# A four-layer graph network on one core: another fixed order for every engine, bound checks inside the work graph, and one input load moved behind four adjacency tiles

## The chip, the cores and the metric

The kernel runs on one core of one Trainium2 chip. The metric is the device time of one execution in microseconds. A core has five engines that run their own instruction queues: the tensor engine (PE in the profile, its weight loads PEld), the vector engine (DVE), the scalar engine (ACT), GpSimd (POOL) and the sync engine (SP), which here only issues transfers. An engine works its queue in the order in which the program was written; a semaphore makes an instruction wait for another engine or for a transfer. Three runs of the kernel before took 4156.73, 4158.40 and 4158.55 us; the median is 4158.4 us.

## The reference

The input `x` is 16 batches of 1024 nodes with 256 features in float32; `adj` is one 1024 x 1024 integer adjacency matrix for all batches. Four layers follow each other, and each adds to `x` what it computes from `relu(layernorm(x))`:

```python
h = jnp.maximum(_layernorm(x, axis=-1), 0.0)
x = x + _L0_gnn_ref(h, adj, L0_gnn_W, L0_gnn_a)   # graph attention, 1 head, relu
...
x = x + _L1_gnn_ref(h, adj, L1_gnn_W, L1_gnn_a)   # graph attention, 1 head, elu
...
x = x + _L2_gnn_ref(h, adj, ...)                  # dot-product attention, 8 heads of 32, masked, then norm, feed-forward, norm
...
x = x + _L3_gnn_ref(h, adj, L3_gnn_W, L3_gnn_a)   # graph attention, 4 heads of 64, elu
```

In a graph attention `e[i,j] = leaky_relu(src[i] + dst[j])`, with `src` and `dst` from `h W a`; where `adj` is zero the weight is none; a softmax over `j` then weights `h W`. Layer 2 takes the scores from queries and keys instead.

## The kernel before

**Tiles.** A batch's 1024 nodes are 8 tiles of 128 (`NT`), in two halves of 4 (`NH`, `TH`). Stages are pairs of layer and batch, 64 in all; the list `order` (L1845 to L1850) runs layer 2 of one batch beside layers 1, 3 and 0 of others, so that stages with different needs overlap.

**The softmax without its maximum.** Exponentials are taken straight, as sums and products of `exp` of source and target. That is right as long as the values stay within bounds. The kernel therefore collects sums and minima in small tiles (`gat_seen`, `inv_seen`, `degree`, `below`), compares them with the bounds after all work (L1990 to L2004), and adds up the broken ones in `bad`. Every engine then loads `bad` into a register (L2013) and jumps over a second, general implementation (`tc.If(found > 0)`, L2014), which runs only where a bound was broken.

**The work graph.** No engine's order is written in the code. `op(...)` (L810) makes a node with its engine, a planned cost in us, a rank, the function that emits its instructions, the nodes it comes after, and the buffers (`Hold`) that it takes and ends. The tensor engine's nodes that the prediction speaks of are these; behind each stands its tile name in the profile:

- `scores` of `dot_item` (L1595, tile `sc`): four products of 32 rows side by side, one per head; planner form 132. It takes two of three pairs of PSUM banks (`"u": Ring(3)`, L967).
- `values` (L1628, `acc<-pe`) and `totals` (L1658, `sums<-pe`) of `dot_item`, `values` and `totals` of `pair_item` for layer 3 (L1477 `acc<-p`, L1502 `sums<-p`): four products of 32 columns side by side; form 32.
- all others use the whole array, form None: `values` of `gat_item` for layers 0 and 1 (`av`), projections (`pm`), transpositions (`tp`, `tps`, `tpo`, `tpv`, `tpr`, `tp_mask`).

Between `scores` and `values` lie two exponentials on ACT (L1613) and two products with the mask on DVE (L1621). Before `totals`, GpSimd issues a transfer that adds one tile of weights onto another (L1647, `pe<-pe`). In the feed-forward of layer 2, GpSimd computes each row's `rstd` (L1054, L1055), ACT scales (L1758), and PE transposes (`tp<-y`).

**The planner.** `forward` (L842) plays the graph: for each engine, `choose` (L824) looks at all nodes that could begin, and among those that could begin within `SLACK` = 0.5 us of the earliest takes the one of the lowest rank. Costs, hand-over delays (`DELAY`) and the cost of a change of PE form (`SWITCH`) are constants. The ranks come from the table `RANKS`, three characters for each node; `play` (L944) uses it where its length fits the number of nodes, and otherwise plans from the ranks in the code:

```python
            if len(RANKS) == 3 * len(ops):
                digits = [DIGITS.index(c) for c in RANKS]
                best = forward([(x * 90 + y) * 90 + z for x, y, z in zip(digits[::3], digits[1::3], digits[2::3])])
```

The nodes' functions are then called in the played order, and that is the order in which each engine's queue is written.

**The first transfers.** SP issues the two halves of batch 0, the eight adjacency tiles of 512 KB each (L724), then the two halves of batch 1 (L725), then weights.

Of the kernel before, what the change touches and what calls it, by code (L numbers as in the profile page):

```python
# [26 lines left out]
F32 = mybir.dt.float32  # L27
BF16 = mybir.dt.bfloat16
U8 = mybir.dt.uint8
I32 = mybir.dt.int32  # L30
AF = mybir.ActivationFunctionType
ALU = mybir.AluOpType
# [15 lines left out]
    "#+;#TX#$I#U9#U3#&X#%h#WX#)4#Wc#&>#$b#U)##w##W$5o##o##Z##D##b#$'#$-##t##$#$:##r##y##G##Q#$F#$>#/4#$N#$R##x#%-#%^"  # L48
    "#$o#'S#'T#&F#&a#%g#&$#'%#&{##T#$|##?##@#%F#SZ##B#%+##>##S#$f##c##M##a##L##]##9##v##i##z##|##u##^#$@#$)##n#$0#$4"
    "##U#oi#-@##V#sX##F##X#$^##=##_#%e##P#)h##{#$<##q#$`#/3#$&#$P##m#$3#$8#$J#$,#$9#$K#$1#*e#%r##%##j#$a#&4$0;#Cy$0r"  # L50
    "#RB#Cx#%|#']#**#&@#)g#([#'q#%m#&]#&7#%v##8#$=##}#$G##-#$L#$_#$j#$M##)#$E##p#$]$$T#'?#%a$Mo#%5#$n#$U#%L#%9#%}#%R"
    "##(#$C#%%#$c#%8##Y#&L#%7#xt#%S#'V#]n#%l#$5$%C#%V#%E#0W#%0##l#&+#$i#&,#%n#(o#)v#)V#D,#%t#$v#$r#$S#%$#%##%'#$O#$d"
    "#$H#$6#)z##4#K5#$+#&I#%?#%Y#(8#YI#(A#<Z#$A#&;#$l#%x#&1#Au#$7#(s#%,#$;#%.#%T#%z#%O#&:#DW#d-#&Q#&A#)W#%s#'H#DU#'P"
    "#'E#&0#(2#(I#(4#'r#*d#e6#&=#,6#k8#&m$Fk$Pc#($#$x#>b#$w#$Z#%3#5Q#$T#&8$@{##J#%X##O#Gr#({#%:#'K#$h#&c#'8##,#&[#%="
    "#T+#$u#&`#V9#%&#'-#%*#JZ#SB#%/#%i##C##5#%w#us##2##H##N#$s#$.#$k##e##;#$e#')#%P#&l#%<##d#$*#$##vC#%K#XB#*|#$B#%G"
    "##A$/b#&6##1#%`#&D#((#%]#%I#%{#&%##0#%_#%Q#&9#&##&)#D=##7#FF$&r#&C#%d#&.##6#)0#&B#+4#O)##3##[#&Y#%@#&g#;b$&?#e'"
    "#4O#%2#&Z#&*#(y##/#%j$/i#&&#'&#di#&p#&/#&f#&M#&|#'.#('$5w#'*#(%#&N#$2#'6#&3#&d#&R#&K#&U#&o#&V##.#DD#&E#&q#M9#'="
    "#&<#&n#eH#'D#',#w'$0(#'X#'C#&z#'J#&h#'@$6t#U@#'[#';#'A#%;#(-#'x#a}#DE#kw#'W#%p#'_#N[#&r#(>#Sm#&u#)G$.4#)P$.3#&e"
    "$Ip#'d#ma#tD#);$Pa$Ph$PQ$K?#&i#'I#&s#'N#&v#'2#&j#%A$D+#&P#&H#0A#%k#(D$JC#'p#'>#'a#&x#&_$JO#G;#O/#'5#'L#%1#'k#0>"
    "$78#(P#ip#'e#'7#kv#P)#d`$Ms$1j#'g#(G#Pd#(l#)@#(E$?$#(c#0.#'w#'s#(p#'G#)E#'}#''#(^#(&#'|#(6#UK#(/$@J#'#$@O#'y#()"  # L60
    "#ku#$Q#'v#$/#Il#.W#B1#(:#(.$>1#)3#4/#Ix#4.#(5#(L$;V$>D##k#(1$9##'u#))#(d#)%#)^#*=#)_#)t##g#'R#'j#(##(,#'U#(9#'i"
    "#(n#(B#(V#(W#&'#(*#'m#*n#)8#)1#(}#;4#)y$$:#(x#C,#(i#(Y#(h#(_#(z#)m#(U#&?#)b#(g#(k#*K#(j$*_#(f#J@#*2#)F#Ah#,[$*9"
    "#*,#*7#-z#<c#)*$LG#)=#)<#++#)M#*:#-(#(v#)B#*+#)i#:q#*1#+9#2y#)?#)Q#+J#)D$$z#*3#,,#*}#)p#)U#;Y#'h#)a#$Y#+<#*9#)S"
    "#)[#*##)$#*&#*R#+%#*H#)w#*[#,r#->#*`#+-#.S#)(#)c#)O$$u#)#$+S#s|#)R#),#/M#)+#,f#*G#+H#*p#*c#(H#*%#*E#*8$,R#*a#*4"
    "#*V#*-#+0#Q5#*k#,U#*q#+*#*@#(@$OJ#*l#-$#*j#*M#)u#qU#+N#,B#*y#K%#-g#+L#*f#*O$P,#*N#*r#+(#*_#)n#,u#j{#-'#+5#+1#IV"
    "#*o#+f#*t$3%#,k#.##h6#+?#'1#-,#,I$2J#,j#+e#L}#,b#+x#+8$2)#E7#nl#kn#+O#+##+K#-D#S{#CK#+u#Oy#)l#,*#+>#+Y$<|#+V#CP"
    "#+t#+i#.M$6O#.C#sD#,$#sv$;[#,N#+`$C?#AC#-k#?L#,'#+z#,T#:M#+D#A<#,F#,>#Os#jT#,J#00#+{#g?#+|#)r#+q#+m#+/#*]#1F#,7"
    "#/[#*U#L^#,+#q<#+X#-+#,8#.`#,3#/)$-($E##-[$F@#D$#-a$8s#Hh#-w$*S$-z#-p#.B#E##-##.u#Ob$GE#F]#+C#8u#qs#.O#.T#-u#L+"
    "#-&#.e#;g#/1#,<#.*#ej#n.#)|#j7#,}#-{#.%#-B#]z#-S#-H#-E#-G#.2#)s$#Z#.(#.c#-Z#GY#a5#/G$Ng#-b#/g$Hu#,)#.i#=.#kT#A&"
    "#gi#,&$Ch#ef$D)$Kp#,Y#8h#-f#,i#,2#-t#*<$Cj#(|#,L#,1$Cs#yr#'0#.Z#,^#8g#/U#-2#,4#'<#/##/P$MP#,o#,Z#-m#ym#2H#g=#,{"  # L70
    "#*C#/d#-O#,]#-K#+&#.-#+W#-1#,l#+o#)o#.{#,##-<#,x#-i#+S#-I#-%#/Q#+}#01#)j#-F#-3#-l#.d#*w#.K#.h$;=$/D#-`#-?$F,#.]"
    "#,X#.g#,A#-_$F)$EL$FB$A=#-o#o8#.q#.&#-N$5r$EI$FC#._#-r#-e#W[#(w#.9#)x#-d#/J$/B#-:#,Q#WZ#}i$P7#)J#-Y#-s#9m#)X#2)"
    "#-7#.N#)`#KW#-U#'l#-V#-0#,?#-x#.I#RQ#,v#/?#.>#.$#.j#.'#.A#-}#.l#/%#.V#/o#.?#-X#./#.<#.b#05#/'#``#.=#-6#'(#+h#2|"
    "#MH#-8#.7#/e#.U#g)#/f#.x#15#/s#/2#.^#,K#/I#,W#,M#Ha$P`#g[#yg#,a#/`#.v#.Y#04#/q#/;#,m#/W#.X#+v#/@#+y$K>#+r#/b#It"
    "#,s#,t$'z#0r$GX#.:#,w#,_#,z#.8#+P#-;#9-#-J#-W#Yt#.m#0S#Ys$>x$(]#.y$9$#)f#+M#$[#(r#,5#*.#*)#,P#*?#*A#,R#$W#*F#*I"
    "#*J#*Q#*>#9e#*P#)9$Kf#+6#nk#+3#+'$3l$F0#+Q#*T#,D#(`#+,#,O#(;#+$#-A#,V#h/#-.#*^#*S#*g#*{$L{#)K$3Y#)T#+a#+n#+=$)E"
    "#+I#+g#+E#+2#+[#Ba#8G#,-#>R#)6#)5#+)#-|#,@$3n#.,#.R#.6#.J$N;#.H#.G#-n#.f#;y#/$#<&#1M#]b#/5#UU#/>#.Q#.t#).#`W#]T"
    "#/Z#zN#0+#-]#*z#/m#1%#/.$7:$Nv#/}#,H#1U$EV#/O#/E#Nt#/z$(B#0&#,:#,S#*$#D5#/u#0x#C/#0i#0{$-f$Mm#-v#u'$+[#'$#0M#0L"
    "#/_##'#N<#I[#.z#3w#):#0;$?F#0(#0P$8h#NP#DY$PU#/,$@X#/t#.}#::#YZ#+R#0'#0n#/h#/v#0F#+G#/=#HG#32#03#/j#C_#/i#-j#0I"
    "#/S#18#/^#/T#3?#.5#1C#z,#HS#0?#0o#6w$-0#1A#61#1k$;Q#1$#0u#0q#/y#/<#1m#1N#0m#/B#0<#0,#2L#26#0##0l#0J#0B#14#0|#/F"  # L80
    "#0]#0V#0[$+k#0O$+f#0a#3n#.+#/D#.w#06#/p#Xr#29#0H#0%#08#0)#0G#0`#0=#0Z#0:$Nn#0y#0k#0e#1,#KY#09#0d#0z#/A#2J#fr#-9"
    "#19$8`#2a#1_#sA#1B#0h#1D#1@#2=#2b#6u#1:#1`#1G#6v#7<#/K#0X#4I$+n#0/#1T#0g#1>#1-$+`#0b#1i#1e#2E#1o#/]$8q#4H#1=#3U"
    "#1}#/c$8K#sh#s?#0K#1W$)u#2C#21#+@#1p#1;#1f#1H#A*#1Q#16#1<#1j#1I#tY$*s#2q#2I#1O#1z#2w#1x$?9#3##/(#1t#1)#1+#1?#2<"
    "#3B#3&#ZZ#2Q#1l$I6#1h#2i#1c#2B#1q#4(#2/#2j#2m#2R$K;#6(#2t#2%#1J#2x#4'#3K#2K#Y1#0t#3c#57#/n#2W$-8#2$#3N#22#1L#3)"
    "#<O#/l#2c#2;#kZ#4D#2_#5A#3M#:u#2D#4F#27#1R#2+#<N#5@#3:#2S#<z$I0$?'#3F#4C#4b#0D#88#2{$Iv#2}#0Q#3>#z0#2z$O'$O&#3$"
    "#4>#39$'1#2e#:s#3/#3j#38#3e#3=#4k#35#4=#3J#5e#3h$5E#4|#Et#+d#*;#3a#2@#5Y#4x#3b#2,#1Z#3Q#4c#4q#79#5T#5'#11#4@#4d"
    "#66#7J#5F#4S#3d#3[#4a#4?#7E$L>#7)#4p#4W#4e#5($;1#;q#6k#5)#23#3+#5$#1n#4i#5d#4^#3y#5;#5^#6H#5h#4-$>P#'B#2'#0_#6h"
    "#0*#4+#3T#3-#<6#37#<v#1a#4g$/'#2##3_#3G#=+#Kb#2Z#{?#2d#4l#nv#2[#4,#2g#4n#:t#56#3W#4J#<r$:C#5>#1b#3(#3.#4L#I=#3{"
    "#N{#3g#l?#7T#59#1^#9;#SA$Iw#2:#58#30#64#13#6Y#12#2^$/*$-7#5i#3l#3Z#8x#2F#7/#1{#*X#3v#/k#1]#8|#1($:x#3`#]k#6]#2X"
    "$JG#2O#6X#2v#3X$9<$.q#2M#07#1[#5E#@Y$)i#tL#ie#40#3C#wv#34#02#3s#T'#3I#4v#3;#3i#2P#0w#5,#2V#x^#3p#77#3O#2]#6P#5P"  # L90
    "#4M$'S#43#7'#4U#0p$,{#4*#6'#3V#3}#3o#4y#5/#2r#5o#5n#5D#6S#3S#5}#5Z#6A#4K#50#5<#67#48#5B#3L#6:#3r#3D#3]#4;#3R#6%"
    "#+j#4f#5_#^{#5H#44#5:$--#4T#33#-R#81#5V#5p#7##^$#3H#41#8;#4t#6L#5y#4m#6-#62#6W#6Q#5k$PR#7N#53#5M#$q#83#2o#5|#2p"
    "#6{#yp$J/$$P#6t#7Q$J0#6M#5S$,]#3u#6s#7H#6+$&=#5`#6K#qc#54#4X#6}#74#|L#6d#Vy#4%#4$#3P#3x#aM#5-#4`#5L#yP#4j#46#j)"
    "#4:#4R#4Z$6p#4{$%>#4P#4z#4##6_#2f$:$#4h#4&#31#5K#4o#5U#6E$Cv#Fk#4w#5w$Np$2&#3f#4G#^z#5g#5m$8a#:T#68#6^#7?#4Y#5W"
    "#45#4E#47#|5$JS#}U$@H#8}#5[#5?$Be#6*#5O$-'#8D#5%#5v#78#5z#2u#9J#7`#6F#6/#6B#}|#5q#rq#70#Ld#87#6N#6J#7$#6r#3m#6x"
    "#+w#6$#6.#6o#76#yf#f>#6b#6l#ww#7(#6O#1S#5a#6f#7%#6e#6[#5f#1Y#7*#73#8-#5X#10#6>#7=#7@#7;#6;#1E#6m#7G#6?#7-#7d#7,"
    "#71#8V#6y#7k$@8#8_#82#91#8$#7l#7Z#7W#[S#7|#8L$51#8[#8I#8`#8i#8m$4M#8^#8W#8P#9,#9W#8c#8p#8##6D#:##8:#Yk#:R$Hn#9&"
    "#<@#9+$2_#;F$+q#V'$D6#8O#<<#?+#??#7S#7q#6U#7I#ET#7U#7]#5s#6j#7V#+p#5N#7b#7R#7}#9)#84#7c#8C#8F#8t#8&#7z#65#7s#7["
    "#7K#7X#7n#*x#6&#7w#7o#9*#7g#EK#8A#8%#6i$(D#7t#7L#6|#8<$&A#-C#8q#8X#,;#6z#8=#8R#8l#7m$J1#9$#>j#Ea#8(#6@#4V#rP#4B"
    "#?=#TB#7r#7P#80#8.#8k#9A#72#9=#8a#8z#9g#Dz#9r#8B#7p#:?#86#'O#9h$%U#:2#tM#-/#8b#8M#9:#:0#8n#9}#&-#Sz#.[#'9#9'#:1"  # L100
    "#t)#;|#(C#Y<#(X#8o#9b#9]#96#9N#9I#;p#9n#8/#8,#;Z#;9#=y#;P#:L#<,#;L#='#4}#9i#9<#9`#(q#=M#WJ#<|#94#(e#9D#9f#6q$Ot"
    "#6p$QC#6Z#:U#7>#9a#W@#:|#8r#m;#8Y#:(#95#9u#8]#:z#8s#9P#{.$(A#9x#=b#:*#7F#8Z#89#8j#9^#7^#8{#8Q#9T###$*-#;*#;8#>)"
    "#@f#>J#5u#@%#8S#7Y#>0#;z#:C#P-#98#;@#<B#9H$Ht#:-#7u#:p#:O#9@#(Z#:%#:=#:A$5b#:.#9V#75#;V#52$%J#zi$B'#:Y#9_##I$-`"
    "##<##&#:H#9t#9q#<V#9M$'J#:G#n]#:o#:c#&w#9U#:`#9/#:_#:Q#:9#9[#:]#8v#jt#:Z$3f$-&#?]#:y#'+#:@#k)#;H#k/#9p#:;#;'#)Z"
# [518 lines left out]
def fast_path(tc, bad, x, adj, l0_w, l0_a, l1_w, l1_a, w_qkv, ln1_g, ln1_b, ln2_g, ln2_b, w1, b1, w2, b2, l3_w, l3_a, out):  # L623
# [13 lines left out]
    with ctx:  # L637
# [186 lines left out]
        def choose(open_ops, time, begin, key, slack):  # L824
# [14 lines left out]
            open_ops[best[1].eng].remove(best[1])  # L839
            return best  # L840

        def forward(rank):  # L842

            time, form, held = [0.0] * 6, 0, {DVE: 0.0, POOL: 0.0}
            ready = [0.0] * len(ops)
# [1199 lines left out]
```

## Time and profile before

| what | value |
|---|---|
| median of three runs | 4158.4 us |
| the profiled execution, its own time | 4158.92 us |
| its span, first to last instruction | 4157.2 us |
| granted PE clock, mean | 0.996 |
| PE busy | 4080.8 us (98%) |
| DVE, ACT, POOL busy | 3123.5, 2316.4, 1255.7 us |
| first PE instruction; last of the layers | 8.63 us; ends 4140.87 us |
| last DVE instruction of the layers | ends 4145.10 us |
| `bad` written | 4148.44 us |

The profile gives each engine's instructions with start and length, what ended the idle time before each, and the names of the tiles. A float32 product appears as two matmul records, so `scores` and `values` are eight records each. Records of PE overlap, and their ends are modelled; the time that an item takes is therefore read from start to start, from its first record to the first of the next item. Queue instructions, such as branches, loads of a register and drains, do not count as busy.

### The profile page before, as it was taken

What the parts mean: (1) busy time and instruction counts of PE and PEld (TensorE: products, weight loads), DVE (VectorE), ACT (ScalarE), POOL (GpSimd) and SP (SyncE); (2) the same over time, 40 slices, a digit from 0 to 9 for tenths busy, and PEclk for the clock granted to TensorE, in tenths of its full rate; (3) what the DMA queues carried; (4) which work ended last, traced back from release to release, by engine and by line L of the source; (5) the groups of instructions that cost most, each with busy time, mean ns of one, the idle gap of its engine ahead of it and who ended that gap; (6) DMA issues with size and microseconds to landing.
All of it is one profiled execution on the core that took longest, in us unless ns stands there. A gap on an engine that the chain in (4) does not pass through costs nothing. (4 is left out here: it accounts for less than half of the span.)

```text
span 4157.2 us, 67132 instructions
## 1 busy us (share of the span) xinstructions
PE 4080.8 (98%) x25993; PEld 2150.9 (52%) x25993; DVE 3123.5 (75%) x5580; ACT 2316.4 (56%) x4235; POOL 1255.7 (30%) x2153
## 2 busy tenths in 40 slices
PE   8999999999999999999999999999999999999998
PEld 7735364553646535465454654546545465465433
DVE  7477867778676886767867678686787767859697
ACT  5564655646466464654646546475564655666452
POOL 3323141413324233142322423223232232423231
PEclk9999999999999999999999999999999999999999
DMA  3181814518155181641716317163271632736361
GB/s 126 25 174 32 188 37 107 108 47 173 37 128 107 36 163 42 140 89 47 152 42 145 84 45 154 42 146 83 51 148 42 144 85 58 146 83 126 74 141 47
DMA packets 106565, 398.91 MB, mean 96 GB/s; under 512 B 11272, under 2 KB 47488, under 8 KB 73472
## 3 DMA queue, kind: packets, MB, share of 16 engines
q0 software_dynamic: 46080, 302.01, 36.8%
q1 hardware_dynamic: 59744, 92.03, 6.6%
q8 instruction: 206, 3.38, 0.3%
q14 instruction: 119, 0.97, 0.1%
q10 hardware_dynamic: 416, 0.52, 0.0%
HBM read 107.87 MB, written 18.21 MB: 30 GB/s over the span
## 5 line engine op out<-in xcount | busy, mean ns | idle before, releaser
L1621 DVE TENSOR_TENSOR pe<-pe,mask 128x1024 f32<-128x1024 f32 x1024 | 1199.7, 1219 | 198.2 <-ACT pe L1613 195.0
L1613 ACT ACTIVATE pe<-sc 128x1024 f32<-128x1024 f32 x1024 | 996.6, 1022 | 299.8 <-PE sc L1599 252.6
L1383 PE MATMUL av<-v,p 128*128 128x257 f32 x4096 | 950.4, 382 | 10.5 <-ACT o L1406 6.8
L1383 PEld LDWEIGHTS av<-v,p 128*128 128x128 f32 x4096 | 758.8, 190 | 195.6 <-issue 59.1
L1445 DVE SCALAR_TENSOR_TENSOR p<-r,e,mask 128x1024 f32<-128x1024 f32 x512 | 622.5, 1274 | 100.3 <-DMA r<-kept 94.1
L1599 PE MATMUL sc<-qT,kT 32*128 32x512 f32 x4096 | 620.0, 641 | 6.8 <-ACT pe L1613 5.3
L1630 PE MATMUL acc<-pe,v 128*32 128x512 f32 x4096 | 535.7, 604 | 2.6 <-DVE pe L1621 1.9
L1647 POOL DMA_DIRECT2D pe<-pe x256 | 226.0, 883 | 980.9 <-PE acc L1630 667.2
L1080 POOL TENSOR_SCALAR rstd<-stats 128x1 f32<-128x1 f32 x512 | 157.8, 308 | 1039.4 <-ACT xn L1074 633.6
L1479 PE MATMUL acc<-p,v 128*32 128x512 f32 x4096 | 468.1, 593 | 0.0
L1599 PEld LDWEIGHTS sc<-qT,kT 32*128 32x128 f32 x4096 | 187.6, 183 | 387.5 <-ACT pe L1613 179.9
L1103 PE MATMUL pm<-l_wx,hT 128*128 128x259 f32 (+1 forms) x1536 | 368.4, 387 | 1.3 <-DVE y L1552 0.6
L1366 DVE SCALAR_TENSOR_TENSOR p<-r,e,mask 128x512 f32<-128x512 f32 x512 | 348.6, 743 | 15.3 <-DMA r<-kept 14.4
L1081 POOL TENSOR_TENSOR rstd<-rstd,minus_half 128x1 f32<-128x1 f32 x512 | 340.1, 664 | 42.6
L1103 PEld LDWEIGHTS pm<-l_wx,hT 128*128 128x128 f32 x1536 | 285.1, 190 | 82.9 <-issue 15.1
L1054 POOL TENSOR_SCALAR rstd<-stats 128x1 f32<-128x1 f32 x256 | 148.6, 580 | 465.0 <-DVE stats L1051 459.8
L1479 PEld LDWEIGHTS acc<-p,v 128*32 128x32 f32 x4096 | 131.3, 110 | 296.3 <-issue 280.6
L1660 PE MATMUL sums<-pe,pick 128*32 128x512 f32 x2048 | 270.5, 600 | 5.6 <-DMA pe<-pe 5.4
L1630 PEld LDWEIGHTS acc<-pe,v 128*32 128x32 f32 x4096 | 96.6, 108 | 337.7 <-issue 200.1
L1157 ACT ACTIVATE xn<-x,stats 128x256 f32<-128x256 f32 x256 | 125.8, 505 | 227.9 <-DVE stats L1051 223.1
L1503 PE MATMUL sums<-p,e 128*32 128x512 f32 x2048 | 249.3, 594 | 1.4 <-ACT v L1246 0.6
L1055 POOL TENSOR_TENSOR rstd<-rstd,minus_half 128x1 f32<-128x1 f32 x256 | 232.1, 907 | 21.4
(124 smaller groups left out, 4211.6 us busy)
## 6 DMA issues: line engine op xcount, KB each, us to landing
pe<-pe POOLq DMA_DIRECT2D x256, 1024.0 KB, 8.8
r<-kept SPq DMA_DIRECT2D x64, 512.0 KB
x<-in_x_dram SPq DMA_DIRECT2D x32, 512.0 KB
x<-offsets POOLq DMA_DIRECT2D x32, 512.0 KB, 5.3
y<-offsets POOLq DMA_DIRECT2D x32, 512.0 KB, 5.9
out_dram<-x SPq DMA_DIRECT2D x64, 256.0 KB
r<-kept SPq DMA_DIRECT2D x62, 256.0 KB
edges<-in_adj_dram SPq DMA_DIRECT2D x8, 512.0 KB
```

The source lines that it names most:

```text
L1081: nc.gpsimd.tensor_tensor(rh.t, rh.t, minus_half, ALU.pow)
L1103: nc.tensor.matmul(dst, lhsT=lhsT[:, k, :], rhs=rhs[:, k, :], start=(k == 0), stop=(k == KC - 1))
L1366: nc.vector.scalar_tensor_tensor(ph.t[:, j % each, :], rh.t, s.e[:, j, H + h : H + h + 1], mask[:, j, cols], ALU.max, ALU.mult)
L1383: nc.tensor.matmul(avh.t[:, : s.hs + 1], lhsT=phs[part].t[:, j % each, i * P : (i + 1) * P], rhs=s.v[:, j, h, :], start=(j == 0), stop=(j ...
L1445: nc.vector.scalar_tensor_tensor(ph.t[:, hh, :], s.rh[hp].t[:, hh, :], s.e[:, j, col : col + 1], mask[:, j, :], ALU.max, ALU.mult)
L1479: nc.tensor.matmul(acc[n].t[(2 * hh + part) * W : (2 * hh + part + 1) * W, :], lhsT=s.v[:, jj, h, part * W : (part + 1) * W], rhs=p, start ...
L1503: both(lambda jj, n, hh, h, p: nc.tensor.matmul(sums.t[(2 * n + hh) * W : (2 * n + hh + 1) * W, 0, :], lhsT=s.e[:, jj, 2 * H + h : 2 * H + ...
L1599: nc.tensor.matmul(scs[pair].t[:, hh, :], lhsT=s.kh.t[r0 : r0 + D2, g, j * P : (j + 1) * P], rhs=s.qh.t[r0 : r0 + D2, g, cols], start=True ...
L1613: lambda pair=pair: nc.scalar.activation(part(pair), scs[pair].t, AF.Exp, scale=SCALE2),
L1621: lambda pair=pair: nc.vector.tensor_tensor(part(pair), part(pair), masks(), ALU.mult), [ex], tiles=True,
L1630: nc.tensor.matmul(head(acc, i), lhsT=s.v[:, j, g * QUAD + i, :D2], rhs=ph.t[:, i, :], start=(j == 0), stop=(j == NT - 1))
L1660: nc.tensor.matmul(head(sums, i), lhsT=pick[:, g, :], rhs=th.t[:, i, :], start=first, stop=last)
```

## The change

1. **Another table, played in another way.** `RANKS` is replaced as a whole, and `forward` gets `in_order=True`: each engine's nodes are sorted by rank, and only the first one left may begin. The table is then each engine's sequence itself, and no longer a preference.
2. **Other planned costs.** Some twenty constants of the planner change by up to 0.6 us. They change no instruction; the planner uses them for the places in which buffers lie and for the order in which the engines' instructions are interleaved.
3. **The bound checks become nine nodes of the graph.** Six comparisons, now one DVE instruction each that also adds up (instead of a comparison and a minimum), one node `judge`, the PE product and the copy to `bad`. They come after the nodes that collect the values (`seen_ops`), and the table gives each a place.
4. **`load_x(1)`** is issued behind the fourth adjacency tile instead of behind the eighth; the planned arrivals follow.

```diff
 RANKS = (
...
-        load_x(1)
+            if t == TH - 1:
+                load_x(1)
...
-        def forward(rank):
+        def forward(rank, in_order=True):
...
+            turns = [deque(sorted((o for o in ops if o.eng == eng), key=lambda o: rank[o.number])) for eng in range(6)]
...
             for _ in ops:
+                if in_order:
+                    open_ops = [[turn[0]] if turn and not missing[turn[0].number] else [] for turn in turns]
                 at, o = choose(open_ops, time, begin, rank, SLACK)
+                if in_order:
+                    turns[o.eng].popleft()
...
-                    result = forward(rank)
+                    result = forward(rank, in_order=False)
...
-                add = op(DVE, 0.39, rank + 0.9, add_one, [o, inv], takes=[mh], ends=[oh, ih], tiles=True)
+                add = op(DVE, 0.51, rank + 0.9, add_one, [o, inv], takes=[mh], ends=[oh, ih], tiles=True)
...
-        x_in = {b: [arrival(at) for at in places] for b, places in {0: (6.0, 7.0), 1: (21.0, 22.0)}.items()}
-        edges_in = [arrival(9.0 + 1.35 * t) for t in range(NT)]
+        x_in = {b: [arrival(at) for at in places] for b, places in {0: (5.7, 8.9), 1: (15.6, 16.9)}.items()}
+        edges_in = [arrival(10.2 + 1.28 * t + (2.7 if t >= TH else 0.0)) for t in range(NT)]
...
+        def verdict(seen_ops, checks, rank):
+
+            def count(i, seen, bound, within):
+                held = small.tile([P, 3 * B], F32, tag="held", name="held", bufs=1)[:, : seen.shape[1]]
+                nc.vector.tensor_scalar(held, seen, bound, 0.0, within, ALU.add, accum_out=ok[:, i : i + 1])
+
+            return [op(DVE, 0.26, rank + i, lambda i=i, c=c: count(i, *c), seen_ops) for i, c in checks]
+
+        counted = verdict(seen_ops, list(enumerate((
...
+        ))), at - 40.0)
+        within = 2 * (3 * B + B + NT)
+
+        def judge():
+            nc.vector.tensor_reduce(broken[:, 0:1], ok, AX.X, ALU.add)
+            nc.vector.tensor_scalar(broken[:, 0:1], broken[:, 0:1], within - 0.5, None, ALU.is_lt)
+
+        judged = op(DVE, 0.32, at - 32.0, judge, counted)
+        counth = banks("count")
+        summed = op(
+            PE, 0.15, at - 31.0,
...
+            ), [judged], takes=[counth],
+        )
+        op(DVE, 0.12, at - 30.0, lambda: nc.vector.tensor_copy(bad, counth.t[:1, 0, :1]), [summed], ends=[counth])
         play()
-
-
-        checks = ((gat_seen[:, 0, :], GAT_HIGH, ALU.is_le), (gat_seen[:, 1, :], GAT_LOW, ALU.is_ge),
...
-            nc.vector.tensor_scalar(held, seen, bound, None, op)
-            nc.vector.tensor_reduce(ok[:, i : i + 1], held, AX.X, ALU.min)
...
-        nc.tensor.matmul(count[:1, :1], lhsT=broken[:, 0:1], rhs=broken[:, 1:2], start=True, stop=True)
-        nc.vector.tensor_copy(bad, count[:1, :1])
```

## The prediction

> **What bounds the kernel now.** I read the page's busy line first, then the tensor engine's instructions in order of time, its waits, a stretch around its longest wait, and the end.
>
> ```profile
> PE 4080.8 (98%) x25993; PEld 2150.9 (52%) x25993; DVE 3123.5 (75%) x5580; ACT 2316.4 (56%) x4235; POOL 1255.7 (30%) x2153
> PE 26%; DVE 2%; DMA 2%; issue 1%; ACT 1%; POOL 0%; SPq 0%; POOLq 0%; DVEq 0%; ACTq 0%
> ```
>
> PE sets the time; no other engine is over 75%. But a busy PE hides two losses, which the timeline shows (columns: start, length, what, count):
>
> ```profile
> 1000.19 1.07 PE L1630 MATMUL acc<-pe,v 128*32 128x512 f32 x8
> 1001.18 1.14 PE L1599 MATMUL sc<-qT,kT 32*128 32x512 f32 x8
> 1002.25 1.97 PE L1630 MATMUL acc<-pe,v 128*32 128x512 f32 x16
> 1004.00 1.09 PE L1660 MATMUL sums<-pe,pick 128*32 128x512 f32 x8
> ```
>
> Two `values` items follow each other from 1002.25 to 1004.00: 0.875 us each, and over all such pairs the shortest is 0.858. Before a `sc` an item lasts 0.99, and a `sc` before `acc` 1.07. So a change of form costs. Taking start-to-start times of all items over the whole trace, the usual surplus is 0.213 us on leaving `sc` (form 132), 0.115 on leaving form 32, 0.095 on leaving the full array (`av` before `sc` 1.83 against 1.738 before `av`). I counted the changes: 1374, of which 509 leave 132, 569 leave 32 and 295 leave None: 108.4 + 65.4 + 28.0 = 201.9 us. The 4139.4 us from the first PE record to the `count` product are then 3769.2 of plain items, 201.9 of changes and 168.4 of other surplus. Of that 96 us lie in 122 pauses of 0.2 us or more (7.4 of `count` apart): 26 before `acc<-pe` with 21.5 us, 18 before `sums<-pe` with 14.1, 11 before `tp` with 13.0, 18 before `av` with 12.7. The other 65 us are in pieces under 0.2, which I take to be of the items themselves. What an order can win is in these 96 and in the 201.9.
>
> The waits view names the releasers (its sum is smaller, because it ends an instruction late by the model):
>
> ```profile
> PE tp L1096 <- ACT y L1758: 10.0, 8, 2.7
> PE count L2003 <- DVE broken L2001: 7.2, 1, 7.2
> PE av L1383 <- ACT o L1406: 6.8, 11, 1.4
> PE sums L1660 <- DMA pe<-pe: 5.4, 9, 1.9
> PE sc L1599 <- ACT pe L1613: 5.3, 6, 3.3
> ```
>
> The longest pause of PE, 5.33 us at 2290.5:
>
> ```profile
> 2288.19 5.21 POOL L1055 TENSOR_TENSOR rstd<-rstd,minus_half 128x1 f32<-128x1 f32 x1
> 2288.34 4.63 DVE L1621 TENSOR_TENSOR pe<-pe,mask 128x1024 f32<-128x1024 f32 x4
> 2293.43 0.51 ACT L1758 ACTIVATE y<-y,rstd 128x256 f32<-128x256 f32 x1 [4.11 <-POOL rstd L1055]
> 2294.91 2.08 PE L1599 MATMUL sc<-qT,kT 32*128 32x512 f32 x4 [3.26 <-ACT pe L1613]
> ```
>
> A one-column GpSimd operation of 0.58 us (median) lasted as long as four mask products of DVE ran one behind another. ACT stood behind it, and PE behind ACT.
>
> The end:
>
> ```profile
> 4144.41 0.69 DVE L1565 TENSOR_TENSOR x<-x,y 128x512 f32<-128x512 f32 x1
> 4148.29 0.15 DVE L2004 CAST bad<-count 1x1 int32<-1x1 f32 x1 [0.37 <-PE count L2003]
> L2014 PEldq COMPARE_BRANCH  x1: 3475/3475/3475, 4149.1 to 4149.1; - x1
> L2041 POOLq DRAIN  x3: 40/107/6726, 4149.3 to 4156.9; - x3
> ```
>
> The checks stand between the last addition (4145.10) and `bad` (4148.44). Then all engines load it (0.5 us) and branch, and GpSimd's drain of 6.7 us, begun only after its branch at 4149.3, sets the end. The last packets of the output land at 4148.5, so the output doesn't.
>
> [...]
>
> **Part by part**, against the span of 4157.2 us; the median of the runs is 1.2 us above it.
>
> *Is the table used at all?* It has 12,289 triples, the old one 12,280, and the graph gains nine nodes (six counts, judge, product, copy). The lengths match, so yes.
>
> *Form changes.* Sorted by the new table, PE's nodes give 1326 changes: 511 leave 132, 540 leave 32, 274 leave None. 108.8 + 62.1 + 26.0 = 196.9 us: **-5.0**. Nearly every `sc` stands alone in both orders; three stretches of PSUM banks don't admit two in a row without an exponential between.
>
> *Pauses.* For each PE item that depends on an earlier PE item through other engines I added up the PE work in between (its lead), in both orders. The short leads get longer: `sc` to its `values` has a 5% point of 4.30 us before and 5.16 after, a least one of 1.93 and 3.65; `acc<-pe` to its `sums` 9.34 and 9.89, with 61 leads under 10 us before and 31 after. But pauses before `values` hardly follow the lead: with the surplus that each lead had in the trace, the new leads give 43 us where there were 42.8. The classes: `sums<-pe` 23.9 to 22 (-1.9); `tps` close behind its `sums`, three leads under 0.5 us cost 5.1 us, one is left (-3.4); `tp` to the up projection, six leads under 1.5 us cost 3.5, two are left (-2.3). Against: four `tpo` now directly follow their `tps`, with a reciprocal of 0.26 us and two hand-overs between, about 0.6 us each (+2.4); one projection directly behind its transposition, with a 1.0 us copy between (+1.3), and some shorter leads to `qT` and `kT` (+0.9). Sum -3. What the sequences of DVE, ACT and GpSimd bring I can't read from leads. Bounds: nothing, and half of the 96 us. One sign: DVE's uninterrupted runs of two-input operations of 6 us or more, by planned cost, are 106 before and 97 after, so GpSimd is shut out a little less. I take -15, a sixth: **-18** in all, from -60 to +20.
>
> *The checks inside.* Six counts of about 0.26 us, judge and copy are some 2 us of DVE, placed 34 to 53 nodes before its end, some 40 to 60 us ahead. Between 4080 and 4100 DVE is now idle for 7.3 us, waiting for `r<-kept`; from 4100 to 4130 it is busy without a gap, while PE runs there without a pause: its last weights are ready at 4132.9 and used at 4135.8. Two us may be covered or eat that margin: **0**, at most +2. The PE product (0.2 us) waits for judge, with only layer 3's items behind it.
>
> *The tail.* GpSimd's last work ends at 4080.9; with `bad` written some 40 us before the end, its branch and drain lie under layer 3. PE branches at 4140.9 and is done by 4145. DVE ends its addition at 4145.10, loads (0.54), branches (0.08)[...]: 4149.3. From the end of the drain to the end of the program took 1.1 us: 4150.4, so -6.7. Were GpSimd's drain still last, only the checks' own 3.34 us would go. I take **-6.5**.
>
> *The start.* Two transfers of 512 KB ahead of the fifth adjacency tile, issued in 1.66 us, delay the last four tiles by about 2.6 us (two planned spacings) and bring batch 1 earlier by the same reasoning about 5 us. The second half's masks are needed only by the second half of the first stage; PE is idle 3.0 us between 8.6 and 35, waiting for masks of the first tiles, and its new order puts projections first, behind the weights' fill of 2.1 us on DVE instead. **0**, from -3 to +2.
>
> Sum: -5.0 - 18 + 0 - 6.5 + 0 = -29.5. Span 4127.7, time 4129 us.
>
> **The rivals.**
>
> *A, above (45%):* 4129, from 4110 to 4142.
>
> *B, the pauses halve (22%):* -48 for them: 4157.2 - 59.5 + 1.2 = 4099. For it: exact sequences with planned costs nearer to the trace (0.51 for an addition that takes 0.48 and 0.08; 3.455 for a product that takes 3.453). Against: the pauses at short leads are few.
>
> *C, pauses only move (23%):* GpSimd's lock-out and a DMA landing of 8.8 us are not in the order; then the changes of form and the tail remain: 4158.4 - 11.5 = 4147.
>
> *D, slower (8%):* GpSimd is shut out at more feed-forwards. There are 32 halves with four `rstd` each before one transposition; they now cost PE 10 us in all, 0.3 us a half. If every second one lost 3.3 us (the mean of the four longest pauses near a `tp`: 5.33, 3.14, 2.49, 2.27), that is 53 - 10 = +43, less 11.5: 4190. It decides from about 0.7 us a half. Against it: DVE's long runs become fewer.
>
> *E, the table is not used (2%):* the lengths would not match and the code's ranks would be planned; slower by an unknown amount.
>
> **How the numbers follow.** About 0.2%, 8.3 us, is what a measurement can tell from no change. Faster: A, B and three quarters of C, 0.84; same: the rest of C and a little of D, 0.07; slower: 0.09. The range from 4090 leaves out a quarter of B, and to 4152 D and E; inside lies a little over 8 in 10. A alone: 4110 to 4142.
>
> **What would show it.** Form changes counted in the new trace: 1326. `bad` written some 40 us before the last addition, GpSimd's long drain before the end, and the end about 5 us behind DVE's last addition instead of 12. Pauses of 0.2 us and over sum to about 78 us. Wrong, if GpSimd's `rstd` waits grow, if pauses before `acc<-pe` rise above 21.5 us, or if the first `av`, now at 28.96, starts over 2 us later.

## The result, and the profile after

The changed kernel takes **4166.5 us** (median of 20 runs, 4158.4 to 4171.8); the kernel before, on the same chip, 4158.8 (20 runs). The ratio is 1.0019, 95% interval [1.0013, 1.0026]: 7.7 us slower, where 29 us faster was forecast. Its profiled run took 4160.8 us, span 4158.6: 5.7 us under its own median, so that this trace shows only 1.4 us of the loss. A second profile of the same kernel (span 4163.5, below) stands nearer to the median.

The busy line and the chain of the page:

```profile
PE 4077.6 (98%) x25993; PEld 2161.1 (52%) x25993; DVE 3080.7 (74%) x5580; ACT 2277.9 (55%) x4235; POOL 1238.1 (30%) x2153
PE 1%; DVE 0%; DMA 0%; POOL 0%; issue 0%; ACT 0%; SPq 0%; DVEq 0%; ACTq 0%
```

PE still sets the time. The chain breaks off after 1% of the span and tells nothing here. The waits of PE (releaser, us in total, times, longest):

```profile
PE sc L1607 <- ACT pe L1621: 8.8, 6, 3.0
PE acc L1638 <- DVE pe L1629: 8.7, 6, 7.4
PE sums L1668 <- DMA pe<-pe: 8.6, 12, 1.6
PE tp L1104 <- ACT xn L1165: 8.3, 2, 7.9
PE acc L1487 <- DVE p L1453: 6.2, 8, 1.6
```

Before, the list was led by `tp` behind ACT's `y`, which stood behind GpSimd's `rstd` (5.21 us at PE's longest pause); that row has gone from 10.0 us to 4.8. In its place stand `sc` behind the exponential and `acc` behind DVE. The longest pause now lies before an `acc` item. From the timeline around it (columns: start, length, engine, what; idle time before it and its releaser in brackets):

```profile
3790.86 0.95 POOL L1655 DMA_DIRECT2D pe<-pe  x1 [2.02 <-PE acc L1638]
3795.06 0.86 POOL L1655 DMA_DIRECT2D pe<-pe  x1 [3.25 <-PE acc L1638]
3795.60 1.21 POOL L1743 DMA_DIRECT2D y<-offsets  x1
3797.30 0.34 SPq L1331 DMA_DIRECT2D r<-kept  x1
3797.54 1.94 ACT L1621 ACTIVATE pe<-sc 128x1024 f32<-128x1024 f32 x2 [0.93 <-PE sc L1607]
3797.87 1.16 SPq L1335 DMA_DIRECT2D r<-kept  x1
3799.07 1.21 SPq L1331 DMA_DIRECT2D r<-kept  x1
3800.34 4.24 SPq L1335 DMA_DIRECT2D r<-kept  x3
3806.89 1.41 DVE L1374 SCALAR_TENSOR_TENSOR p<-r,e,mask 128x512 f32<-128x512 f32 x2 [9.71 <-DMA r<-kept]
3808.22 2.35 DVE L1629 TENSOR_TENSOR pe<-pe,mask 128x1024 f32<-128x1024 f32 x2
3809.49 2.20 PE L1638 MATMUL acc<-pe,v 128*32 128x512 f32 x6 [7.35 <-DVE pe L1629]
```

Nine transfers are issued within 14 us: two gathers of 1 MB, one addition of the offsets, six loads of `r`. An issue on SP, 0.42 us in the median of all 126 loads, takes over a microsecond. DVE's next instruction in its fixed order needs one of the loads and stands for 9.71 us; the mask products behind it in the same order could have run, since ACT had finished their exponentials by 3799.5, and PE stands 7.35 us for them. The same place in windows of 2 us (length, PE busy, its granted clock, share of the DMA engines, GB/s):

```profile
3802.00:3804.00 2.00, 0.14 (x1) 1.00 0.85 138
3804.00:3806.00 2.00, 0.00 (x0) 0.56 1.05 233
3806.00:3808.00 2.00, 0.00 (x0) 0.50 1.04 324
3808.00:3810.00 2.00, 0.51 (x2) 0.50 1.05 365
3810.00:3812.00 2.00, 2.00 (x10) 0.50 0.99 389
3812.00:3814.00 2.00, 2.00 (x10) 0.50 1.09 317
3814.00:3816.00 2.00, 2.00 (x10) 0.88 1.14 242
3816.00:3818.00 2.00, 2.00 (x11) 1.00 0.74 152
```

The DMA engines are full (shares of 0.85 to 1.14 until 3816), and, what I had not looked for, PE's clock is halved from 3804.2, 2.1 us into the pause, to 5 us beyond it.

The end: the copy to `bad`, the last addition on DVE, and queue instructions of the tail.

```profile
4112.34 0.14 DVE L2030 CAST bad<-count 1x1 int32<-1x1 f32 x1
4151.09 0.69 DVE L1573 TENSOR_TENSOR x<-x,y 128x512 f32<-128x512 f32 x1
L2041 PEldq COMPARE_BRANCH  x1: 3415/3415/3415, 4146.8 to 4146.8; - x1
L2041 POOLq COMPARE_BRANCH  x1: 45/45/45, 4113.1 to 4113.1; - x1
L2041 DVEq EVENT_SEMAPHORE  x1: 21/21/21, 4155.4 to 4155.4; - x1
L2041 SPq EVENT_SEMAPHORE  x8: 17/17/17, 4153.8 to 4156.9; - x8
L2068 POOLq DRAIN  x3: 40/107/6726, 4113.3 to 4158.3; - x3
```

`bad` is written 38.8 us before the last addition begins, GpSimd branches at 4113.1, and its drain of 6.7 us no longer lies at the end. From DVE's last addition to the end of the span it is 6.8 us (12.1 before): 5.3 gained. The last to be waited for is now SP: its output transfers were issued until 4153.1, and it waits for their landing until 4156.9.

**Where the time went.** By the same bookkeeping as in the prediction, from the first to the last item of PE: before 4131.2 us, after 4138.0. Changes of form 201.9 to 197.0 (counted: 1326); pauses of 0.2 us and over 96.4 to 115.2; the small pieces 64.6 to 57.5; plain items the same. PE begins 0.75 us earlier. So PE's stream is 6.8 us longer, of which +18.8 in the pauses.

I followed each pause of 0.2 us and over back through its releasers, to a transfer, or to a GpSimd operation that took well over its usual time, or to an engine that was simply busy (us of PE's pauses):

| root | before | after | after, second profile |
|---|---|---|---|
| a transfer | 12.9 | 44.5 | 46.2 |
| GpSimd held up | 19.4 | 13.3 | 15.6 |
| chain through a busy DVE | 28.8, 7.0 of it the old `count` | 9.0 | 8.9 |
| chain through ACT | 5.1 | 2.2 | 2.5 |

What the new order was for, it does: the pauses from the engines' own order and from GpSimd fall by 22 us (46.3 to 24.5, `count` apart). The transfers add 31.6. Without `count` the rows sum to 59.2 us before and 69.0 after; the other 9 us of the +18.8 stand in no row, and experiment 3 comes back to them.

The page's line of the gathers (the transfers that add one tile of weights onto another) hides what happened to them, before and after:

```profile
pe<-pe POOLq DMA_DIRECT2D x256, 1024.0 KB, 8.8
pe<-pe POOLq DMA_DIRECT2D x256, 1024.0 KB, 8.7
```

The median didn't move. But of 256 gathers, 26 took over 10.5 us to land before, 55 after (over 12 us: 7 and 26); SP's issues of over 1 us are 18 and 48. What they met can be counted. In the first 6.9 us after its issue (the shortest landing of all) 22 gathers before and 39 after had 0.25 MB or more of SP's transfers (loads of `r` and the like) moving beside them. Of these, 7 and 27 took over 10.5 us: 20 of the 29 additional late ones. Their median landing was 9.6 and 11.6 us, that of the others 8.7 and 8.4. Gathers overlapped each other about as often in both (243 and 250 pairs). A rival is that DVE's two-input operations hold up GpSimd when it issues a gather: in the first 2.5 us such operations filled 0.92 of the time for the late gathers after the change and 0.87 for the others (before: 0.91 and 0.91), so this does not tell them apart.

### The profile page after: what moved, and what is told of

Its sections match the earlier page's. It is cut to its first block, busy times and chain, and to the rows that moved or that the text cites. A ratio compares the mean times of both kernels' runs of the same rounds, so it can differ in the third digit from the quotient of the medians.

```text
span 4158.6 us, 66917 instructions
## 1 busy us (share of the span) xinstructions
PE 4077.6 (98%) x25993; PEld 2161.1 (52%) x25993; DVE 3080.7 (74%) x5580; ACT 2277.9 (55%) x4235; POOL 1238.1 (30%) x2153
## 5 line engine op out<-in xcount | busy, mean ns | idle before, releaser
L1453 DVE SCALAR_TENSOR_TENSOR p<-r,e,mask 128x1024 f32<-128x1024 f32 x512 | 626.1, 1273 | 108.6 <-DMA r<-kept 106.2
L1638 PE MATMUL acc<-pe,v 128*32 128x512 f32 x4096 | 548.3, 608 | 9.1 <-DVE pe L1629 8.7
L1487 PE MATMUL acc<-p,v 128*32 128x512 f32 x4096 | 493.5, 593 | 6.3 <-DVE p L1453 6.2
L1088 POOL TENSOR_SCALAR rstd<-stats 128x1 f32<-128x1 f32 x512 | 155.7, 304 | 1003.9 <-ACT xn L1082 591.9
L1374 DVE SCALAR_TENSOR_TENSOR p<-r,e,mask 128x512 f32<-128x512 f32 x512 | 356.7, 742 | 30.5 <-DMA r<-kept 29.6
L1089 POOL TENSOR_TENSOR rstd<-rstd,minus_half 128x1 f32<-128x1 f32 x512 | 346.4, 677 | 42.6
L1062 POOL TENSOR_SCALAR rstd<-stats 128x1 f32<-128x1 f32 x256 | 137.1, 536 | 550.5 <-DVE stats L1059 539.2
L1487 PEld LDWEIGHTS acc<-p,v 128*32 128x32 f32 x4096 | 141.9, 110 | 305.0 <-issue 263.8
L1511 PE MATMUL sums<-p,e 128*32 128x512 f32 x2048 | 264.3, 593 | 1.2 <-DVE p L1453 1.1
L1408 DVE RECIPROCAL inv<-av 128x1 f32<-128x1 f32 x256 | 41.3, 164 | 277.9 <-PE av L1391 269.9
L1107 ACT ACTIVATE hT<-tp 128x1024 f32<-128x1024 f32 x160 | 163.6, 1023 | 133.7 <-PE tp L1104 133.0
```

Source lines behind the costliest of these rows:

```text
L1089: nc.gpsimd.tensor_tensor(rh.t, rh.t, minus_half, ALU.pow)
L1374: nc.vector.scalar_tensor_tensor(ph.t[:, j % each, :], rh.t, s.e[:, j, H + h : H + h + 1], mask[:, j, cols], ALU.max, ALU.mult)
L1453: nc.vector.scalar_tensor_tensor(ph.t[:, hh, :], s.rh[hp].t[:, hh, :], s.e[:, j, col : col + 1], mask[:, j, :], ALU.max, ALU.mult)
L1487: nc.tensor.matmul(acc[n].t[(2 * hh + part) * W : (2 * hh + part + 1) * W, :], lhsT=s.v[:, jj, h, part * W : (part + 1) * W], rhs=p, start ...
L1511: both(lambda jj, n, hh, h, p: nc.tensor.matmul(sums.t[(2 * n + hh) * W : (2 * n + hh + 1) * W, 0, :], lhsT=s.e[:, jj, 2 * H + h : 2 * H + ...
L1638: nc.tensor.matmul(head(acc, i), lhsT=s.v[:, j, g * QUAD + i, :D2], rhs=ph.t[:, i, :], start=(j == 0), stop=(j == NT - 1))
```

## The experiments

**Theory T**: the table was found in a plan that gives every transfer a fixed time, so it packs transfers into the same moments; on the chip they share the DMA engines, land late, and in a fixed order everything behind a late one stands. **R1**: the checks or the moved load cost the time. **R3**: the engines' own order costs it.

**1. The parts of the change, one at a time.**

The new table of turns, played in order and with the change's planned costs, the rest as before. The code of this section shows only the lines that matter:

```diff
+RANKS = (the new table, without its last nine)
-            if t == TH - 1:
-                load_x(1)
+        load_x(1)
```

> The new table of turns alone: the checks stand behind the graph as before, and the second input is loaded at its old place. If the new turns bunch the transfers (theory T), the whole loss lies in them: the changes of form give -5, the pauses +19 or more, and without the shorter end (-5.3) the time is some 13 us above before, about 4172, ratio 1.003. If the turns are good and the checks or the moved load cost the time (rival R1), it is below before: about 4150, ratio 0.998.

The checks inside the graph, the rest as before:

```diff
-        play()
-        checks = ...
+        counted = verdict(...); judged = op(DVE, 0.32, ...); summed = op(PE, 0.15, ...)
+        play()
```

> Before with the nine check operations inside the graph, the turns and the load of the second input as before. Theory T: the end becomes 5.3 us shorter and nothing else changes, about 4153.5, ratio 0.9987. Rival R1: about 4160 or more, because the checks delay layer 3.

The load alone:

```diff
-        load_x(1)
+            if t == TH - 1:
+                load_x(1)
```

> Before with only the load of the second input moved behind the fourth adjacency tile; the sequence of every other instruction is that of before. Theory T and my prediction's step: within 3 us of before, ratio 1.000. Rival R1: 5 us or more slower, from masks that come late in the first stage.

And the changed kernel once more:

> The changed kernel once more, beside the other three on one chip, with a second profile. Ratio 1.002 (4166.5). Theory T: the pauses of the tensor engine of 0.2 us and over again sum to 110 us or more, and some 40 of them go back to transfers; the places may differ, since the transfers' landing times differ from run to run. If instead the engines' order itself makes the pauses (rival R3), the same pauses stand at the same places with the same lengths.

| kernel | median us | ratio to before | 95% |
|---|---|---|---|
| order alone | 4172.5 | 1.0025 | [1.0013, 1.0036] |
| checks alone | 4153.0 | 0.9984 | [0.9976, 0.9992] |
| load alone | 4158.9 | 0.9998 | [0.9990, 1.0007] |
| the changed kernel | 4165.0 | 1.0015 | [1.0008, 1.0021] |

R1 falls: the load does nothing, the checks gain what the end showed (before itself: 4159.6 here). The whole loss, 13 us, is in the new order. One part of my last expectation missed: most of the long pauses of the second profile stand at the same places with almost the same lengths (7.4 us before the same `acc`, 3.2 and 3.6 before the same two `tp`), though one grew from 2.9 to 5.8 us. I had thought that transfers would scatter. They repeat from run to run, so this did not tell T from R3.

**2. Shorter gathers**, in both kernels. The gather moves half of its bytes, so the sums of two heads in every odd tile are left out.

```diff
-                    out=th.t.rearrange(...), in_=ph.t.rearrange(...), accum_op=ALU.add
+                    out=th.t[:, : QUAD // 2, :].rearrange(...),
+                    in_=ph.t[:, : QUAD // 2, :].rearrange(...), accum_op=ALU.add
```

> Before, but each accumulating gather moves only two of the four heads (512 KB instead of 1 MB); the sums of the other two heads of the odd tiles are left out. Theory T (transfers that run at the same time make each other late, and the new turns let more of them run at the same time): before has 12.9 us of pauses that go back to transfers, so the gain is 10 us at most and about 5 by the clock besides: 4145 to 4155. Rival R3 (the turns of the engines): the same gain here as in the changed kernel.

> The changed kernel with the gathers halved in the same way; the sums of two of the four heads of the odd tiles are left out. Theory T: of 44 us of pauses that go back to transfers most vanish, and with them most of the stretches at half clock: 30 to 45 us less, 4122 to 4137, below before with half gathers by 15 us or more. Rival R3: some 5 to 10 us less, and still above before with half gathers.

Before falls to 4148.0 (ratio to before 0.9967 [0.9955, 0.9979]), the changed kernel to **4123.2** (0.9908 [0.9893, 0.9923]). The gain is 12 us in one and some 43 in the other; R3 wanted the same in both. With gathers that land in 4.6 us, the changed kernel is 25 us faster than before. Some 6 of these are the end, which the checks alone gave, so the order's part is some 19. In its trace the pauses with a transfer at their root fell from 44.5 to 17.0 us, only 0.7 of it the gathers':

```profile
pe<-pe POOLq DMA_DIRECT2D x256, 512.0 KB, 4.6
L1453 DVE SCALAR_TENSOR_TENSOR p<-r,e,mask 128x1024 f32<-128x1024 f32 x512 | 626.0, 1273 | 109.0 <-DMA r<-kept 107.1 <-PE sums L1511 1.2 <-PE acc L1487 0.2
L1374 DVE SCALAR_TENSOR_TENSOR p<-r,e,mask 128x512 f32<-128x512 f32 x512 | 356.8, 743 | 19.0 <-DMA r<-kept 18.1 <-PE sc L1607 0.5 <-ACT mask L1906 0.3
```

DVE still waits 125 us for `r` (in the changed kernel 106.2 + 29.6): most of these waits PE never sees.

**3. The halved clock.** In every trace PE's clock is 1.00 but for stretches at 0.50, whose lengths are multiples of 3.413 us. Their beginnings lie on one grid of that width: in the changed kernel's trace at 517.21 us and then 60, 220, 517, 675, 735, 823, 963 and 1026 widths later, each to within 0.01 us; before, at 2294.93 us and 151 and 229 widths later. I cut each trace into windows on that grid. By the share of a window in which PE stood (gaps of over 1 us between its instructions; twelve traces of the kernels here, without the first 20 us: the records of the clock begin at 18.2 us before and at 15.5 us in the changed kernel), the next window was at half clock in:

```
share of the window idle    next at half clock
0.65 and over               60 of 60
0.60 to 0.65                 8 of 9
0.50 to 0.60                13 of 29
0.30 to 0.50                19 of 95
under 0.30                  12 of 14253
```

The ends of the records are modelled, so the shares are only as sharp as that. Before had 17.1 us at half clock ahead of its last item, the changed kernel 44.4; PE worked in all of the 17.1 and in 35.8 of the 44.4. A `values` item takes 1.71 us there instead of 0.88, so about half of this work time is lost: an estimate of 8.5 us before and 17.9 after, 9 us more. That is the size of what stood in no row of the table above. **Theory C**: each long pause is paid for a second time. Test: fill long pauses with work that changes nothing (the changed kernel also has such products with zero weights, not shown).

```diff
+                n, place = warm("tp")
+                        if n and place == 2 * u + k:
+                            for _ in range(n):
+                                nc.tensor.transpose(tph.t[:, k, u * P : (u + 1) * P], ident, ident)
                         nc.tensor.transpose(tph.t[:, k, u * P : (u + 1) * P], src()[...], ident)
-                for pair in pairs:
+                n, _ = warm("sc")
+                for pair in [0] * n + list(pairs):
```

> The checks inside the graph at the old turns, and in four of the tensor engine's longest pauses (three transpositions in feed-forwards and one score product) work that changes nothing: 8 to 12 transposes of the identity into the place that the late transposition then overwrites, and the first score pair four times more. Theory C (a window of 3.4 us in which the tensor engine stands for over 0.6 of it is followed by one or two windows at half clock): the clock stays at 1.00 up to the last item, the pauses end when they ended before, and the time falls by up to 13.65 / 2 = 6.8 us against the same kernel without this work, to about 4147. If the granted clock has nothing to do with the pauses, the half-clock windows remain, and the time is that of the checks alone (4153) or more by the work put in (6 us).

> The changed kernel with such work in seven of its pauses (three transpositions, two score products, one values product with zero weights, one values product of a GAT layer with zero weights). Theory C: of 44 us at half clock some 30 vanish, 15 us of work less those stretches in which the tensor engine stood anyway: about 4155, 10 us below the changed kernel. If the clock does not follow the pauses: 4166 or more.

The checks-alone kernel at its longest pause, without and with the filling:

```profile
2296.00:2298.00 2.00, 0.00 (x0) 1.00 0.29 57
2298.00:2300.00 2.00, 1.31 (x4) 0.78 0.32 66
2300.00:2302.00 2.00, 2.00 (x10) 0.50 0.97 197
2302.00:2304.00 2.00, 2.00 (x14) 0.50 1.28 258
2304.00:2306.00 2.00, 2.00 (x16) 0.52 0.70 98
```

```profile
2296.00:2298.00 2.00, 2.00 (x14) 1.00 1.00 205
2298.00:2300.00 2.00, 2.00 (x12) 1.00 0.57 115
2300.00:2302.00 2.00, 2.00 (x10) 1.00 0.26 53
2302.00:2304.00 2.00, 1.82 (x18) 1.00 1.03 209
2304.00:2306.00 2.00, 2.00 (x24) 1.00 0.97 197
```

The clock follows the pauses: filled, the three stretches are gone, and one of 3.4 us appeared at another pause that was not filled. The time hardly followed: 4152.1 (0.9980 [0.9973, 0.9987]) against 4153.0 without filling, where 4147 was expected; both ratios lie within each other's intervals. Item by item the filled kernel gains 3.2 us across the pause shown and 0.8 across the next, and loses about as much in pieces of 1 to 1.6 us at other pauses. In the changed kernel it brought nothing: 4167.2 (1.0013 [1.0004, 1.0022]); at four places the stretch is gone, at others a pause moved, and PE's work at half clock fell only from 35.8 to 28.0 us, worth 4 us by the estimate above. So C holds for the clock, and an item's time doubles there. What a stretch costs the whole kernel, these runs show at one place only: 3.2 us for 6.8 at half clock.

**4. The table searched again, in a plan in which transfers share.** The kernel's plan is a function in its own code. I let the transfers in it go through one server, each for its size over the rate that the trace gives it, and searched by local moves (one operation a few places up or down in its engine's turns, kept if the planned end falls), starting from the change's own table.

```diff
+                if o.moves:
+                    time[QUEUE] = max(time[QUEUE], at + cost + 1.0) + o.moves
+                    end = time[QUEUE] + max(0.3, o.delay - 1.0 - o.moves)
...
-            gathered = op(QUEUE, 5.6, at[0] - 4.0, lambda: None, [issued], ends=[ph])
+            gathered = op(QUEUE, 5.508, at[0] - 4.0, lambda: None, [issued], ends=[ph], delay=1.0)
-                        delay=3.6 if H == 1 else 4.2,
+                        delay=3.6 if H == 1 else 4.2, moves=0.8532 if H == 1 else 1.7172,
... (the same for the stores, the inputs and the offsets)
+RANKS = (another table)
```

> The changed kernel with another table of turns, found by local moves from its own table in a plan where transfers share one server: gathers take it for 5.5 us, the offsets' additions 2.8, r loads 1.72 or 0.85, outputs 1.73 and inputs 3.46 (sizes over the rates of the trace, 8% added). In this plan its own turns end at 4173 us and the new ones at 4093, with 1338 changes of form. Theory T: transfers no longer meet at the same time, the pauses that go back to them fall from 44 us to under 15 and the half-clock windows with them; the time falls by 40 to 70 us against the changed kernel, to 4097 to 4127, and below the checks alone (4153). Rival R3 (the engines' own order, or delays that no plan knows): 4150 or more.

The control has the change's plan and code, and only another table:

> A control: as much more search by the same moves from the same table, but in the change's own plan, where every transfer takes a constant time. There the end goes from 4086.0 to 4085.7; in the plan with a shared server the new turns would end at 4160 instead of 4173. Theory T: within 12 us of the changed kernel, 4155 to 4172. If searching longer is what helps, it falls as far as the other new table does.

and both again with other random moves:

> A second table searched in the plan with the shared server, from the changed kernel's table with other random moves: planned end 4095.9 (the first 4092.9), 1336 changes of form. If the shared server is what made the first one faster, this one is as fast: 4130 to 4145. If the first was luck among tables, it lies where the constant-delay tables lie, 4148 or more.

> A second control, searched in the constant-delay plan with other random moves: planned end 4085.7 there (as the first control), 4162.5 in the plan with a shared server (first control 4159.7, the change's own table 4173.1). If the shared plan ranks tables rightly, some 3 us above the first control, about 4151, and under the changed kernel; if equal tables of the constant plan scatter, anywhere between 4145 and 4170.

| table | its end in the fixed plan | in the shared plan | measured | ratio to before, 95% | pauses from transfers | gathers over 12 us |
|---|---|---|---|---|---|---|
| the change | 4086.0 | 4173.1 | 4166 | 1.0019 [1.0013, 1.0026] | 44.5 | 26 |
| fixed plan, searched on | 4085.7 | 4159.7 | 4148.2 | 0.9983 [0.9976, 0.9991] | 34.7 | 17 |
| the same, other moves | 4085.7 | 4162.5 | 4164.8 | 1.0015 [1.0008, 1.0021] | 56.1 | 16 |
| shared plan | 4122.0 | 4092.9 | 4137.4 | 0.9959 [0.9945, 0.9972] | 26.6 | 8 |
| the same, other moves | 4121.1 | 4095.9 | **4131.4** | **0.9938 [0.9925, 0.9952]** | 19.7 | 10 |

The busy line of the last kernel, and its waits:

```profile
PE 4061.5 (98%) x25993; PEld 2151.8 (52%) x25993; DVE 3082.0 (75%) x5580; ACT 2274.9 (55%) x4235; POOL 1239.1 (30%) x2153
PE sums L1723 <- DMA pe<-pe: 12.5, 9, 3.5
PE tp L1159 <- ACT y L1821: 9.6, 2, 5.8
PE av L1446 <- ACT o L1469: 5.5, 10, 1.0
```

Both tables of the shared plan beat both kernels, by 17 to 26 us against before, and by 10 to 19 against the old order with the checks inside (0.9984), which the first control only equals; the row of `acc` behind DVE's mask product has fallen from 8.7 us to 1.4. These runs were taken on several chips, so kernels are compared by their ratios to before. Three tables with the same end in the fixed plan (within 0.3 us) lie up to 15 us apart by them, and the two shared ones, 35 us later in it, are the fastest: that plan ranks nothing here, and part of the change's loss is which table was taken. By the fixed plan the old order, with the checks inside, ended at about 4142, some 56 us behind the change; on the chip it is some 14 us ahead. The profiles of the two controls are their slowest runs (4153.6 and 4175.7), so the last two columns show them worse than their medians. My expectations were too high in size and, for the first control, wrong: 4155 to 4172 expected, 4148 measured. The shared plan promised 77 to 80 us against the change's table and gave 25 to 34 by the ratios; 20 to 27 us of pauses still go back to transfers, with the gathers themselves now first. It also puts the first control ahead of the second by 2.8 us where 13 were measured. So the shared plan tells the two kinds of tables apart, two tables against three, but not the rank within a kind. The gathers that had 0.25 MB or more of SP's transfers beside them fit it: 39 in the change, 23 and 25 in the controls, 17 and 15 with the shared plan. (The kinds also differ in planned costs, from which buffers get their places; that was not tried apart.) And that it puts the change's table behind the old order hangs on a margin that I chose: without the 8% added to the transfers it puts the change's table at 4143.9 and the old order at 4150.1, with it at 4173.1 and 4166.5.

## Why the prediction was wrong, point by point

- **The table is used, 1326 changes of form**: right; 197.0 us measured, 196.9 forecast. (The parts listed there sum to one less, as for before; the last change is that to the `count` product.)
- **The checks inside cost 0**: right. Alone they give -6.6 us (4153.0 against 4159.6); their trace has 6.05 us from DVE's last addition to the end instead of 12.05, and PE's stream is no longer than before.
- **The tail, -6.5**: right in mechanism, 5.3 in size. I let the end fall 1.1 us after the drain of the engine that came last, DVE. DVE's event came at 4155.4, but SP, which I had dismissed because the output landed early before, waits until 4156.9. Its last issues stretch (one took 1.7 us). The forecast of 4149.3 for DVE holds, besides its load and its branch, the 3.56 us between DVE's branch and its next event in the trace of before; after the change they are 3.25. What fills them no run here shows, nor what PE's branch (3.475 us before, 3.415 after) and GpSimd's drain (6.726 us in both) consist of.
- **The start, 0**: right; load alone is at 0.9998.
- **The pauses, -18: this step failed**, by 37 us (-18 forecast, +18.8 measured in pauses of 0.2 us and over; the smaller pieces gave back 7.1, which I had left as they were). Two parts of it were wrong in different ways. The leads counted PE work between an item and the earlier item that it hangs on, and priced a lead by what such leads had cost before. That keeps the time of the transfer inside the lead constant. The leads were longer by the count (31 `sums` leads under 10 us against 61), but a longer lead doesn't cover a gather that lands late, and twice as many did (55 over 10.5 us against 26, the median unchanged): pauses before `sums<-pe` went from 14.1 to 19.0 us, where -1.9 was forecast. The other part, -15 for the sequences of DVE, ACT and GpSimd that "I can't read from leads", had the right sign for what it named: chains through DVE, ACT and GpSimd fell from 46 us (the old `count` apart) to 24.5. It left the fifth sequence out. I had the orders of SP and of the transfers and never asked which transfers would now be in flight together.
- **A pause was priced at its own length.** The clock was not looked at; the page of before shows PEclk at 9 in every slice, since stretches of 3.4 or 6.8 us vanish in slices of 104 us; the mean clock of 0.996 was the sign. Each window in which PE stood for 0.65 or more was followed by one at half clock (60 of 60 in experiment 3), so such a pause also slows what follows. Of the +18.8, some 10 us are PE standing and, by the estimate in experiment 3, some 9 are this slower work.
- **GpSimd's lock-out** (rival D) is not the cause: 19.4 to 13.3 us. The traces show it in the 256 feed-forward operations on `rstd` (L1055 before, L1063 after; medians 0.581 and 0.573 us): 84 took over twice the median before and 59 after, and DVE's operations with two inputs (`TENSOR_TENSOR`, `SCALAR_TENSOR_TENSOR`) ran for at least 0.69 and 0.68 of each. Of the 45 and 64 with no such operation beside them none took over 0.60 us. D had the right side for another reason.
- **Rival C came nearest** ("a DMA landing of 8.8 us" is among what is "not in the order"): it named the thing that decided, and then took it as a cover that stays, not as one that grows. Its 4147 is what checks and forms would give if the pauses had only moved.
- **The signs**: of the three that I said would show it wrong, pauses before `acc<-pe` did rise (21.5 to 27.3 us); the first `av` starts 1.9 us earlier, not later; the waits for `rstd` did not grow.

With gathers that land in 4.6 us the two kernels stand 25 us apart, near the 29.5 of the sum; without the end it is some 19 against the 23 for forms and pauses. The sum priced the order as if transfers didn't make each other late.

What stays open: why tables of one plan scatter by 15 us; what a half-clock stretch costs on the whole; and how much of the two shared-plan tables' remaining 20 to 27 us a plan could still take away.

## What to carry to other kernels

When an order is fixed by a search, read the plan for what it holds constant: here the search spent its freedom there, and there the chip disagreed. List the transfers that the new order has in flight together, not only how long each has until it is needed; a transfer's landing time in the old trace is a price for the old order. An engine that works in order and waits for one late transfer stops everything behind it (here DVE for 9.71 us, with mask products behind it whose exponentials were done, and PE 7.35 us for these), so a table needs slack exactly where it shares.

## What the runs showed that I had not expected

- PE's granted clock goes to 0.50 for one to four times 3.413 us (four in the second control of experiment 4) when it has stood for 0.65 of a window or more, 2.2 us (60 of 60 windows; 7.35 us of waiting from 3802.1: 10.2 us at half clock; 2.7 us from 2807.2 before: 3.4 us). It stayed at 1.00 in the three pauses of the checks-alone kernel that had led to half clock, once they were filled with idle matrix work.
- A gather of 1 MB lands in 6.9 us at the least, 8.7 in the median and up to 14.2 in the changed kernel; of 512 KB, 4.5 at the least. From the two least times an estimate: 0.5 MB of these accumulating gathers costs 2.4 us, about 215 GB/s, beside a fixed part of some 2 us.
- An issue of an `r` load on SP lasts 0.32 us at the least, over a microsecond where the DMA engines are full (3797.9 to 3804.6, above), and up to 2.1 in the changed kernel: SP's issue time is a sign of the congestion.
- Late transfers repeat from run to run: two profiles of the changed kernel have the same long pauses, most of them within 0.5 us.
